# Layer 0's output stores on ScalarE's queue, and more yields between the steps of its attention

## The chip, the cores and the metric

The kernel runs on one core of a Trainium2 chip. The metric is the device time of one execution in microseconds; the time of a kernel is the median of several runs. One profiled execution goes with it, and its rows are in microseconds from the start of its span.

## What is computed

The input is `x` of shape 4 x 48 x 256 x 256 in float32. Four layers follow, each `x = x + layer(group_norm(x))`. Only layer 0 is touched by the change. Cut to what matters it is:

```python
qkv = conv1x1(gn(x), qkv_w)                 # 48 -> 144 channels
qkv = depthwise3x3(qkv, dw_w)
q, k, v = split(qkv)                        # each 48 x (256*256), one head
q, k = l2_normalize(q), l2_normalize(k)     # over the pixels
attn = softmax(q @ k.T * temperature)       # 48 x 48 for each image
x = x + conv1x1(attn @ v, proj_w)
```

Layer 1 is a set of recurrences along rows and columns, layer 2 and layer 3 are convolutions with 8 x 8 Fourier patches.

## The kernel before

Layer 0 never forms `q`, `k` or `v`. The 48 x 48 attention of an image depends only on correlations of the input with shifted copies of itself, so a first stage (the matmuls at L367 and L371) sums these over each image, and VectorE gathers statistics (L407). For each image a generator, `attention`, turns the sums into one small set of weights `wu[b]`: it contains `statistics` (matmuls `ps_mu`, `ps_va`, `ps_wt`), seven pairs of blocks (`ps_u`, `ps_y`), the reduction `half`, and small steps `ps_t`, `ps_l`, `ps_m`, `ps_w`, `ps_x` that end by writing `wu[b]`. Each `yield` in it is a place where other work may be put between two steps; the kernel's schedule is written out by hand, and instructions stand on each engine in the order in which the Python code issues them. One call of `next(steps)` runs the generator to its next yield. For images 0 to 2 the steps are spread between the matmuls of the next image's correlations, one call for every four column pairs, 64 calls for an image. Before the change the generator has 28 yields.

The last image has no next correlations. Its first steps run directly after the loop, and the rest runs in the output stage, one step after each row group.

The output stage applies `wu[b]` to the image as a 3 x 3 convolution in Winograd form over row pairs. It is 32 jobs, 8 for each image, each of 32 rows of the image in two halves `hf`:

- `load_out` (L459) brings the rows of a job into one of two buffers `xos`, two DMAs of 49 partitions x 18576 bytes, issued on SP two jobs ahead.
- `transform` (L475, L476, L478) is four pieces on GpSimd that write the tile `to` of the next job (two buffers).
- `out_rows`, four times in a job, makes two products of 48 matmuls each (`po`, L490, three buffers). ScalarE copies half of the first product to SBUF (`c2`, L502); VectorE adds and subtracts (L504, L505) and so empties that buffer; with the second product it finishes the rows (L507, L508) and gathers statistics for layer 1 (L510); four ScalarE copies (L514) put the rows into the stage tile of the job in layer 1's order.
- `store` (L523) writes the stage tile to the scratch tensor `x1` in four DMAs, each 48 channels x 64 runs of 128 bytes. They were issued on SP.

The order of issue in a job is: the loads for two jobs on, then for each of the four row groups one transform piece of the next job, one `out_rows` and one attention step of the last image (from job 1 on), and last the four stores. So on SP the loads of a job stand behind the stores of the job before.

Of the kernel before, what the change touches and what calls it, by code (L numbers as in the profile page):

```python
# [17 lines left out]
B, C, H, W = 4, 48, 256, 256  # L18
# [84 lines left out]
def layer0(k):  # L103
    nc, tc = k.nc, k.tc
    main, first, second = correlations()
    NB, CB = len(main) + len(first) + len(second), 5
    with ExitStack() as ctx:
# [5 lines left out]
        def small(name):  # L113
            return ps_s.tile([128, 512], F32, name=name, tag="small")
# [16 lines left out]
        with ExitStack() as gctx:  # L131
# [74 lines left out]
            def statistics(b, st):  # L206

                mv = sp.tile([128, C, 2], F32, name="mv", bufs=1)
                for c in range(C):
                    nc.vector.bn_aggr(mv[:, c, :], st[:, c].rearrange("p t s -> p (t s)"))  # L210
                    if c % 8 == 7:
                        yield
                ps = small("ps_mu")
                nc.tensor.matmul(ps[:, :C], ones, mv[:, :, 0], start=True, stop=True)
                groups = lambda x: x.rearrange("p (g i) -> p g i", i=3)
                gm = sp.tile([128, C // 3], F32, name="gm")
                nc.vector.tensor_reduce(gm, groups(ps[:, :C]), AX.X, ALU.add)
                nc.vector.tensor_scalar(gm, gm, 1.0 / 3, None, ALU.mult)
                spread = lambda x: x[:, :, None].broadcast_to([128, C // 3, 3])
                d = sp.tile([128, C], F32, name="dv")  # L220
                nc.vector.tensor_tensor(groups(d), groups(mv[:, :, 0]), spread(gm), ALU.subtract)
                nc.vector.tensor_tensor(d, d, d, ALU.mult)
                nc.vector.tensor_tensor(d, d, mv[:, :, 1], ALU.add)
                yield
                ps = small("ps_va")
                nc.tensor.matmul(ps[:, :C], ones, d, start=True, stop=True)
                gs = sp.tile([128, C // 3], F32, name="gs")
                nc.vector.tensor_reduce(gs, groups(ps[:, :C]), AX.X, ALU.add)
                nc.vector.tensor_scalar(gs, gs, 1.0 / 3, GN_EPS, ALU.mult, ALU.add)
                nc.scalar.activation(gs, gs, AF.Sqrt)  # L230
                nc.vector.reciprocal(gs, gs)
                nc.vector.scalar_tensor_tensor(gm, gm, -1.0, gs, ALU.mult, ALU.mult)
                for i, row in enumerate((gs, gm)):
                    full = sp.tile([128, C], F32, name="full")
                    nc.vector.tensor_copy(groups(full), spread(row))
                    dg = sp.tile([C, C], F32, name=f"dg{i}")
                    nc.vector.tensor_tensor(dg, k.ident[:C, :C], full[:C], ALU.mult)
                    if i == 1:
                        bias = sp.tile([C, 1], F32, name="bias")
                        nc.vector.tensor_reduce(bias, dg, AX.X, ALU.add)  # L240
                    for h in range(2):
                        if i == 0:
                            nc.vector.tensor_copy(lw[:, h * HP : h * HP + C], dg)
                        else:
                            nc.vector.tensor_copy(lw[:, h * HP + C : h * HP + CA], bias)
                yield
                ps = small("ps_wt")
                nc.tensor.matmul(ps[:, :P2], lw, wq, start=True, stop=True)
                wt = sp.tile([128, P2], F32, name="wt")
                nc.vector.tensor_copy(wt, ps[:, :P2])  # L250
                yield
                return wt

            def attention(b, st, pa, pb, pc):
# [5 lines left out]
                o = na + nb + 2 * na  # L260
                nc.vector.tensor_copy(cs[:HP, o : o + 4 * CA], pc[:HP, 2 * na : 2 * na + 4 * CA])
                wt = yield from statistics(b, st)
                edge = {"left": 13, "right": 13, "top": 16, "bottom": 16}

# [35 lines left out]
                half = sp.tile([P2, P2], F32, name="half")  # L300
                nc.vector.tensor_reduce(half, ws.rearrange("p m j -> p j m"), AX.X, ALU.add)
                yield
                ps = small("ps_t")
                nc.tensor.transpose(ps[:P2, :P2], half, k.ident[:P2, :P2])
                g = sp.tile([P2, P2], F32, name="g")
# [8 lines left out]
                nc.vector.reciprocal(rn, rn)  # L314
                nc.vector.tensor_scalar(gd, k.ident[:P2, :P2], rn, None, ALU.mult)
                yield
                ps = small("ps_l")
                nc.tensor.matmul(ps[:C, :C], g[:, :C], gd[:, C:], start=True, stop=True)
                at = sp.tile([C, C], F32, name="at")
# [5 lines left out]
                nc.vector.tensor_reduce(mx[:, 1:2], at, AX.X, ALU.add)  # L325
                nc.vector.reciprocal(mx[:, 1:2], mx[:, 1:2])
                nc.vector.tensor_scalar(at, at, mx[:, 1:2], None, ALU.mult)
                yield
                ps = small("ps_m")
                nc.tensor.matmul(ps[:C, :C], at, projT, start=True, stop=True)  # L330
# [82 lines left out]
            for at, (b, h, q) in enumerate(jobs):  # L413
                if at + 1 < len(jobs):
                    ts[at + 1] = load(*jobs[at + 1])
                if h == 0 and q == 0:
                    pa = ps_a.tile([128, 512], F32, name="pa")
                    pb = ps_b.tile([128, 512], F32, name="pb")
                    pc = ps_c.tile([128, 512], F32, name="pc")
                    st = rp.tile([128, C, 8, 6], F32, name="st", bufs=2)  # L420
                t = ts.pop(at)

                def step():
                    for i in range(8):
                        stats(st, h, q, t, range(6 * i, 6 * i + 6))
                        next(once if b == 0 else steps, None)
                        if b == 1:
                            next(once, None)
                        yield

                correlate(b, h, q, t, pa, pb, pc, step())
                if h == 1 and q == 3:
                    borders(pc, rw)
                    if b + 1 < B:
                        rw = load_border(b + 1)
                    steps = attention(b, st, pa, pb, pc)
                    next(steps)
            for _ in once:
                pass
            for _ in range(C // 8):  # L440
                next(steps)

        with ExitStack() as octx:
# [75 lines left out]
            def store(b, u, stage):  # L519
                for hf in range(2):  # L520
                    for c in range(2):
                        n0 = u * RU + hf * RU // 2 + c * RU // 4
                        nc.sync.dma_start(  # L523
                            k.x1[b // 2][:, b % 2, :, :, :, n0 : n0 + RU // 4, :].rearrange(
                                "c k p h n j -> c (k p h) (n j)"
                            ),
                            stage[c * HP : c * HP + C, hf].rearrange("c k p h n j -> c (k p h) (n j)"),
                        )
# [7 lines left out]
            for i, (b, u) in enumerate(jobs):  # L536
                cur = t
                if i + 2 < len(jobs):
                    xs[i + 2] = load_out(i, *jobs[i + 2])
                pieces = []  # L540
                if i + 1 < len(jobs):
                    t, pieces = transform(xs.pop(i + 1))
                for n in range(RU // 4):
                    if pieces:
                        pieces[n]()
                    out_rows(b, u, n, cur, stages[i % 2])
                    if i > 0:
                        next(steps, None)
                store(b, u, stages[i % 2])
# [1049 lines left out]
def network(ctx: ExitStack, tc: tile.TileContext, a):  # L1599
# [35 lines left out]
    k.y3 = [dp.tile([C, H, W], F32, name=f"y3_{b}") for b in range(B)]  # L1635

    layer0(k)
    layer1(k)
    layer2(k)
# [153 lines left out]
```

## Time and profile before

| what | us |
|---|---|
| median of 3 runs | 14373.09 |
| lowest and highest run | 14365.64 to 14403.29 |
| the profiled execution, its own time | 14317.74 |
| its span | 14316.0 |
| TensorE (PE) busy in the span | 13484.9 |
| VectorE (DVE) busy | 7589.3 |
| ScalarE (ACT) busy | 5440.0 |
| GpSimd (POOL) busy | 4000.5 |
| layer 0: correlations | 0 to 1266 |
| layer 0: output stage, first to last product | 1297.85 to 2082.99 |

An engine's busy time counts its compute instructions; issuing a DMA is not counted, so ScalarE or SP can be held up without appearing busy. A row of a timeline gives the start, the duration, the engine, the line of the kernel, the operation with its output and inputs, how many, and in brackets how long the engine was idle before and what ended that. SPq is SP's issuing queue. A line of a table of windows gives the stretch, its length, the busy time and number of instructions of PE, weight loads, DVE, ACT and POOL, the granted TensorE clock, and the DMA engines' share and GB/s.

### The profile page before, as it was taken

What the parts mean: (1) busy time and instruction counts of PE and PEld (TensorE: products, weight loads), DVE (VectorE), ACT (ScalarE), POOL (GpSimd) and SP (SyncE); (2) the same over time, 40 slices, a digit from 0 to 9 for tenths busy, and PEclk for the clock granted to TensorE, in tenths of its full rate; (3) what the DMA queues carried; (4) which work ended last, traced back from release to release, by engine and by line L of the source; (5) the groups of instructions that cost most, each with busy time, mean ns of one, the idle gap of its engine ahead of it and who ended that gap; (6) DMA issues with size and microseconds to landing.
All of it is one profiled execution on the core that took longest, in us unless ns stands there. A gap on an engine that the chain in (4) does not pass through costs nothing.

```text
span 14316.0 us, 409316 instructions
## 1 busy us (share of the span) xinstructions
PE 13484.9 (94%) x177348; PEld 9066.8 (63%) x177348; DVE 7589.3 (53%) x18639; ACT 5440.0 (38%) x11419; POOL 4000.5 (28%) x3769
## 2 busy tenths in 40 slices
PE   9998979999999899999999999997999999899998
PEld 5555657676767655555555555555777777666666
DVE  2334753333545566666666666664555555565554
ACT  0001334422320055555555555553444444232232
POOL 0002760000006544444444444441111111111111
PEclk9999989999999999999999999996999898898888
DMA  3333677766659833333333333325887777787787
GB/s 145 145 145 106 141 138 132 129 149 145 151 145 222 193 44 46 45 46 47 44 48 47 47 48 46 46 40 112 166 166 161 156 162 159 159 167 150 154 161 142
DMA packets 1843543, 1681.08 MB, mean 117 GB/s; under 512 B 1486821, under 2 KB 1588586, under 8 KB 1804634
## 3 DMA queue, kind: packets, MB, share of 16 engines
q1 hardware_dynamic: 1776202, 1378.92, 44.8%
q0 software_dynamic: 65536, 275.97, 12.1%
q8 instruction: 1393, 22.82, 0.8%
q14 instruction: 412, 3.38, 0.1%
HBM read 978.44 MB, written 676.01 MB: 116 GB/s over the span
## 4 chain that ended last, share of the span: by engine, by line
PE 79%; DVE 8%; DMA 6%; issue 3%; POOL 2%; ACT 1%; SPq 1%; DVEq 0%; POOLq 0%; ACTq 0%
PE pc L959 17%; PE p L610 16%; PE pg L1437 8%; PE pb L371 6%; PE py L1365 5%; PE pm L1402 4%; PE pm L1483 4%; PE pa L990 3%; PE pm L1458 3%; PE pb L1015 3%; DMA xo<-in_x_p 2%; PE pm L1340 2%; PE pb L1069 2%; PE pb L1060 2%; PE pa L367 2%
## 5 line engine op out<-in xcount | busy, mean ns | idle before, releaser
L959 PE MATMUL pc<-wg,t 50*64 50x288 f32 x49152 | 3373.3, 405 | 151.7 <-DVE qkv L975 113.2
L959 PEld LDWEIGHTS pc<-wg,t 50*64 50x64 f32 x49152 | 2010.9, 133 | 1459.2 <-issue 318.0
L1377 DVE TENSOR_TENSOR z<-py,meff 64x288 f32<-64x288 f32 x4096 | 1687.6, 451 | 1121.0 <-PE py L1365 1095.4
L1437 PE MATMUL pg<-z,kw 100*64 100x64 f32 x36864 | 1486.9, 238 | 144.6 <-DVE gall L1450 80.1
L1437 PEld LDWEIGHTS pg<-z,kw 100*64 100x64 f32 x36864 | 1336.4, 148 | 347.8 <-issue 158.7
L1053 POOL TENSOR_TENSOR z<-z,gb 128x768 f32<-128x768 f32 x512 | 933.4, 1823 | 2101.4 <-ACT z L1047 1584.7
L610 PE MATMUL p<-carry,wk_down 96*96 96x256 f32 x6120 | 1356.2, 384 | 94.9 <-DVE carry L615 54.9
L975 DVE TENSOR_TENSOR qkv<-pc,c 128x576 f32<-128x576 f32 x1024 | 773.1, 755 | 1230.5 <-ACT c L974 1210.3
L610 PEld LDWEIGHTS p<-carry,wk_down 96*96 96x96 f32 x6120 | 1010.0, 165 | 440.7 <-DVE carry L615 67.8
L778 POOL TENSOR_TENSOR x1in<-carry,x1in 96x256 f32<-96x256 f32 x512 | 435.1, 855 | 2413.3 <-DMA x1in<-x 2215.6
L371 PE MATMUL pb<-t 128*64 128x490 f32 x4096 | 1041.5, 576 | 7.4 <-DMA t<-in_x_t 7.4
L982 DVE TENSOR_TENSOR qkv<-pc,qkv 128x576 f32<-128x576 f32 x1024 | 773.6, 755 | 337.2 <-PE pc L959 309.3
L1450 DVE TENSOR_TENSOR gall<-gall,pg 128x384 f32<-128x384 f32 x768 | 426.0, 555 | 861.9 <-PE pg L1437 654.4
L1365 PE MATMUL py<-wi,xf 48*64 48x144 f32 x16384 | 836.5, 321 | 45.8 <-issue 24.2
L490 PE MATMUL po<-to,wu 49*64 49x256 f32 x12288 | 711.6, 391 | 57.9 <-POOL to L475 50.8
L1415 POOL DMA_DIRECT2D z<-eb x256 | 130.0, 508 | 2245.5 <-DMA eb<-yb 958.1
L908 ACT ACTIVATE xn<-xr,ab 48x1152 f32<-48x1152 f32 (+1 forms) x512 | 716.7, 1428 | 29.7 <-DMA xr<-x 24.8
L1463 ACT COPY gt<-pm 100x512 f32<-100x512 f32 x1024 | 544.4, 591 | 481.8 <-PE pm L1458 479.3
L1402 PE MATMUL pm<-z,mb 64*32 64x396 f32 x6144 | 701.0, 556 | 12.3 <-issue 10.3
L1365 PEld LDWEIGHTS py<-wi,xf 48*64 48x64 f32 x16384 | 536.6, 146 | 264.4 <-issue 148.0
L1448 ACT ACTIVATE gall<-pg 128x384 f32<-128x384 f32 x768 | 378.3, 493 | 854.2 <-PE pg L1437 844.2
L610 PE MATMUL p<-carry,wk_left 96*96 96x256 f32 x3060 | 668.8, 381 | 34.4 <-DVE carry L615 34.4
(213 smaller groups left out, 19427.5 us busy)
## 6 DMA issues: line engine op xcount, KB each, us to landing
t<-in_x_t SPq DMA_DIRECT2D x96, 1666.0 KB
eb<-yb SPq DMA_DIRECT2D x1024, 148.5 KB
z<-eb POOLq DMA_DIRECT2D x512, 297.0 KB, 10.4
xf<-xf SPq DMA_DIRECT2D x512, 224.0 KB
xo<-in_x_p SPq DMA_DIRECT2D x64, 888.9 KB
xr<-x SPq DMA_DIRECT2D x120, 432.0 KB
x<-stage SPq DMA_DIRECT2D x128, 384.0 KB
xin<-x SPq DMA_DIRECT2D x128, 384.0 KB
```

Source lines behind the costliest of these rows:

```text
L371: nc.tensor.matmul(out, left, right, **flags)
L490: nc.tensor.matmul(p[c * HP : (c + 1) * HP, hf, i], wu[b][o, m, dx], t[o, m, c * NP // 2 + n, dx : dx + W], start=(dx == 0), stop=(dx == 2),)
L610: nc.tensor.matmul(pv, wk[name][:, o, :], old[:, :, o : o + N], start=(o == 0), stop=(o == 2))
L908: lambda up=up, rows=rows, half=half, wp=wp, dst=dst, dm=dm, m0=m0, m1=m1: nc.scalar.activation(rows[:, dst, wp, m0 - dm : m1 - dm], src[: ...
L959: nc.tensor.matmul(pc[cc * HP : (cc + 1) * HP, h, :O], j.t[p, which, n, w0 : w0 + HP], wg[p, which, dx], start=(dx == 0), stop=(dx == 2),)
L975: nc.vector.tensor_tensor(j.qkv[:, g // 2, :, g % 2], j.pc[1][:, 0:1, :O].broadcast_to([128, 2, O]), c2, ALU.add)
L982: nc.vector.tensor_tensor(o, j.pc[0][:, :, :O], o, ALU.add)
L1053: nc.gpsimd.tensor_tensor(z, z, gb[:, i : i + 1, :].broadcast_to([128, 8, Q]), op)
L1365: nc.tensor.matmul(py[v * HP : (v + 1) * HP, hf, ii * PASS : (ii + 1) * PASS], xf[p, i, v, :], wi[p, j.ps, :], start=True, stop=True,)
L1377: nc.vector.tensor_tensor(out[:, :, :, v, :], py[p, hf, : 2 * PASS].rearrange("p (i c e) -> p c i e", i=2, e=2), meff[p, j.ps].rearrange(" ...
L1402: nc.tensor.matmul(pb[32 * q : 32 * q + 32, :n], mb, z[:, a : a + n], start=True, stop=True)
L1437: nc.tensor.matmul(pg[e * HP : (e + 1) * HP, kk], k.k3[g][:, (t * GP + kk) * 2 + e, :], z[:, :, t * NP2 + g * GP + kk, :, e], start=True, ...
```

## The change

Two edits. The four stores of a job are issued on ScalarE's queue instead of SP's, in the same place of the program, so behind the last stage copies of the job and ahead of the first copy of the next. And six bare `yield` lines are added to the generator: one ahead of `ps_va`, two ahead of `ps_wt`, one each ahead of `ps_t`, `ps_l` and `ps_m`, so 34 in all; the loop after the correlations runs five steps instead of six, so that `ps_mu` goes into the output stage. From `store` on, line numbers of the changed kernel are higher by 6.

```diff
@@ statistics
                 nc.vector.tensor_tensor(d, d, mv[:, :, 1], ALU.add)
                 yield
+                yield
                 ps = small("ps_va")
...
+                yield
+                yield
                 yield
                 ps = small("ps_wt")
@@ attention
                 yield
+                yield
                 ps = small("ps_t")
...
                 yield
+                yield
                 ps = small("ps_l")
...
+                yield
                 yield
                 ps = small("ps_m")
@@ after the correlations
-            for _ in range(C // 8):
+            for _ in range(C // 8 - 1):
                 next(steps)
@@ store
-                        nc.sync.dma_start(
+                        nc.scalar.dma_start(
                             k.x1[b // 2][:, b % 2, :, :, :, n0 : n0 + RU // 4, :].rearrange(
```

## The prediction

> **What bounds the kernel now.** I read the page for the weight of layer 0 (the lines of layers 1 to 3 are untouched), then the chain that ended last, to find who sets the pace of layer 0's output stage, then SP's issues, one row of the stage in order of time, and the places where TensorE stops. The stage runs from the first product at 1297.85 us to the end of the last at 2082.99: 785.1 us for 32 jobs.
>
> The chain between 1700 and 2030 us (start, length, what) is a loop over the loads of `xo`:
>
> ```profile
> 1706.70 15.90 DMA xo<-in_x_p
> ...
> 2020.75 15.81 DMA xo<-in_x_p
> ```
>
> Between these two lie 13 periods, 314.05 / 13 = 24.2 us per job. TensorE itself needs less, as its column in the table of windows shows (494.95 of 530 us busy, part of that at a slow clock):
>
> ```profile
> 1510.00:2040.00 530.00, 494.95 (x8636) 345.16 (x8632) 347.69 (x542) 190.60 (x453) 385.48 (x259) 0.95 0.64 143
> ```
>
> SP's issues in order of time (start, length held, line, count):
>
> ```profile
> 1369.22 9.80 SPq L523 DMA_DIRECT2D x<-stage  x4
> ...
> 1707.10 21.94 SPq L523 DMA_DIRECT2D x<-stage  x4
> 1729.14 3.12 SPq L459 DMA_DIRECT2D xo<-in_x_p  x2
> 1732.36 19.67 SPq L523 DMA_DIRECT2D x<-stage  x4
> 1752.13 3.09 SPq L459 DMA_DIRECT2D xo<-in_x_p  x2
> ```
>
> The reader is to see that SP is never free: 3.12 + 19.67 us and small gaps make the whole 23 us from 1729.14 to 1752.13. A store moves 3072 runs of 128 bytes, and its issue is long by itself:
>
> ```profile
> L523 SPq DMA_DIRECT2D x<-stage x128: 302/3037/16118, 1323.5 to 2091.4; - x128
> ```
>
> Minimum, median and maximum: the first of four is taken in 0.33 us, each later one waits 3.04 for the one before, and one per job waits 13 to 16 behind the load just issued on the same queue. Without a load ahead four stores hold the queue 9.80 us (at 1369.22). That number is the core of this forecast.
>
> One row of the stage while nothing is short (four rows make a job):
>
> ```profile
> 1735.21 0.59 ACT L502 COPY c<-po 112x512 f32<-112x512 f32 x1 [0.22 <-PE po L490]
> 1735.83 0.69 DVE L504 TENSOR_TENSOR y<-po,c 112x512 f32<-112x512 f32 x1 [0.66 <-ACT c L502]
> 1736.44 0.68 DVE L505 TENSOR_TENSOR y<-po,c 112x512 f32<-112x512 f32 x1
> 1737.75 0.69 DVE L507 TENSOR_TENSOR y<-po,y 112x512 f32<-112x512 f32 x1 [0.63 <-PE po L490]
> ...
> 1738.47 0.43 ACT L514 COPY stage<-y 112x256 f32<-112x256 f32 x1 [2.68 <-DVE y L507]
> 1739.07 1.10 ACT L514 COPY stage<-y 112x256 f32<-112x256 f32 x3 [0.16 <-DVE y L508]
> ...
> 1740.39 0.59 ACT L502 COPY c<-po 112x512 f32<-112x512 f32 x1 [0.23 <-PE po L490]
> ```
>
> L502 to L502 is 5.18 us, so a half-row product takes 2.59 and a job 20.72. ScalarE idles only 0.2 us between the last stage copy (ends 1740.17) and the next L502, and L502 is what lets VectorE empty a `po` buffer. Two more places, a restart of TensorE after a stop, and the longest stall in the last image's attention:
>
> ```profile
> 1723.91 6.63 PE L490 MATMUL po<-to,wu 49*64 49x256 f32 x60 [3.75 <-POOL to L475]
> ...
> 1729.43 0.59 ACT L502 COPY c<-po 112x512 f32<-112x512 f32 x1 [6.82 <-PE po L490]
> ```
>
> ```profile
> 1329.68 20.53 DVE L229 TENSOR_SCALAR gs<-gs 128x16 f32<-128x16 f32 x1
> ...
> 1352.46 0.74 PE L248 MATMUL ps_wt<-wq,lw 48*128 48x96 f32 x2 [19.90 <-DVE lw L245]
> ```
>
> After a stop of 3.75 us, 60 matmuls take 6.63 us, 0.110 each instead of 0.054: the first product ends 5.52 us after the restart instead of 2.59, so a stop costs about 3.0 us on top of itself.
>
> **The change, part by part.** *Stores to ScalarE.* On SP it removes 19.7 to 21.9 us of issue per job. The loads then go out as soon as GpSimd has read the old buffer, about 18 us into a job (4 pieces of 1.10 + 1.10 + 2.39 us), land 14 to 16 us later, and are wanted at the start of the job after next: off the path. Taken alone the period would fall from 24.2 to TensorE's 20.72.
>
> On ScalarE it adds 4 issues per job behind the last stage copy. Queued behind them: the next job's first L502; behind that VectorE's L504 and L505 (in order, so all its later work), and TensorE, which has three `po` buffers. With the end of the job's last product as zero: L507 starts at 0.05, the last stage copy ends at 0.05 + 2.42 = 2.47 (rows above), four stores hold ScalarE 9.80 us to 12.3, L502 starts there instead of at 2.59, and L505 ends 1.91 later (1735.21 to 1737.12), at 14.2. TensorE fills three buffers by 3 x 2.59 = 7.8 and stops until 14.2: 6.4 us. With the slow restart of 3.0 that is 9.4 per job. The rest of the job catches up: at half speed ScalarE and VectorE have 5.5 us for a half-row that takes them 2.6. Period 20.7 + 9.4 = 30.1. Of 32 jobs 31 have a successor to delay: 31 x 9.4 = 292 us.
>
> No row shows an issue on ScalarE. The near row is the same store on SP, 9.80. From below: each is taken in 0.33 as the first of four is, 1.3 us in all, and costs nothing, because the third buffer leaves 3.3 us of slack (12.3 - 2.59 = 9.7 of delay made 6.4 of stop). From above: ScalarE also waits for the fourth store's runs, 9.80 + 3.04 = 12.8, which gives 12.4 per job, 385 us. I take 9.80: same transfer, same runs.
>
> The Trainium skill, "Perfetto Trace Analysis", section "DMA Instruction — HWDGE (DVE, Sync)", says that the issuing sequencer is held until all descriptors of its DMA have been generated; the 0.33 us of the first store speaks for one that is generated after the issue returned, and by the page alone the term would be the 385. "DMA: Bandwidth & Descriptors", section "Issuing engines are not separate DMA queues", says that issuing from several engines saves only the sequencer's issue time, usually small next to the transfer; here that time is 19.7 of 23 us, so the page's "small" does not hold, and by its words the change would be worth nothing.
>
> Would stores still wait for loads, as on SP (19.67)? At a period of 30 us a load goes out at 18 and lands at 32 to 34, so 2 to 4 us into the next job; the stores start at 2.5 and end at 15. They hardly meet, and the longer the period the less. I price this at 0, at most 2 us per job.
>
> *The spacing.* The edited generator serves all images. For images 0 to 2, 34 yields instead of 28 fit the 64 slots; TensorE is busy all through them (320.0 of the 320 us from 400 to 720 us) and other matmuls stand between the steps either way: 0. Dropping one step after the loop saves nothing, as TensorE idles from 1266.4 to 1297.85 for the `xo` buffers, not for `ps_mu`. In the output stage the third image's steps spread over 29 rows instead of 22. Their matmuls stay: about 13 us. Now TensorE stops 19.9 us (above), 2.5 for `half` and 4.0 for the `wu` chain, with three slow restarts 35 us. L229 took 0.175 us elsewhere and here 20.53, until GpSimd's unbroken run of `to` pieces ended. With three steps between, `ps_wt` no longer waits; but the same kind of operation (L218) now stands in job 1, at about 1341, with GpSimd busy to 1350. I put 18 us, between 5 (all hidden) and 35 (as now).
>
> **Sum for the stage:** 663.0 (32 x 20.72) + 3 (first slow start) + 13 + 18 + 292 = 989, against 785: +204 us. The tail stays: the last four stores leave at the same distance from the last row, SP or ScalarE. On the profiled execution's 14317.74 us (span 14316.0) this is 14522. That execution lies 55 us below the median of the three runs, 14373.09; on that median, 14577.
>
> **The rivals.** *Faster:* ScalarE is not held by its issues. Then the stage is 663 + 3 + 13 + 35 (GpSimd busy 18 of 20.7 us, so the lock stays) = 714, 71 us less: 14302. For it: the 0.33 us of the first issue. Against it: 3.04 is the median, with nothing else ahead. It decides below a hold of some 6 us: break-even is (785 - 697) / 31 = 2.8 us per job beyond the 3.3 of slack. *A longer hold:* the fourth store counts, or stores meet the tail of a load: 989 + 93 = 1082, 14670. With every store behind a load (19.67) it would be 31 x 19.3 = 598 and 14880, but the loads' phase, above, excludes that for most jobs. *Nothing to measure:* a hold of 5 to 6 us, where the unblocked loads pay for ScalarE's stops; about 14373. No row lies there.
>
> **How the numbers follow.** The forecast (hold near 9.8) has 0.72, the longer hold 0.14, no change 0.04, faster 0.10. A comparison of this kernel resolves some 0.3%, 43 us. The likeliest case spans +100 to +270: the stall term between 6.5 (a restart without slow clock) and 11 us per job, and 5 to 35 for the attention. The range reaches into the longer hold, 14465 to 14690, and leaves the faster case out.
>
> **What would show it.** Right: ScalarE issues of 3.0 us, three of four, with the store line on the chain; TensorE stopping about 6 us in every job, ended by VectorE's L511 (today's L505); granted clock in the stage well under 0.95; no wait of GpSimd for `xo`; period near 30 us. Wrong: issues of 0.3 us on ScalarE and a period of 21, or an L508 that starts on time; or issues of 13 us there, which would mean that loads and stores collide again.

## The result and the profile after

| what | before | after |
|---|---|---|
| median of 6 runs, us | 14388.19 | 14592.06 |
| lowest to highest, us | 14338.89 to 14457.49 | 14530.67 to 14618.88 |
| span of the profiled execution, us | 14316.0 | 14545.3 |
| layer 0's output stage, us | 785.1 | 960.8 |

The ratio of the times is 1.0128, 95% interval 1.0091 to 1.0165: slower by more than the 0.3% that such a comparison resolves. The stage now runs from 1297.4 to 2258.2 us and is 175.7 us longer. The span is 229.3 us longer; the other 54 us lie outside the stage, in code that the change does not touch. The span without the stage was 13530.9 us before and 13584.5 after, and between 13504.4 and 13637.1 in the ten kernels below, which have the same code there. It varies by some 130 us from one execution to the next, so the length of the stage is the sharper measure here, and the medians the fairer one of the whole.

The table of windows over the stage, first of before, then of after, shows what became of TensorE (columns: stretch, length, busy time and number of PE, weight loads, DVE, ACT, POOL, granted clock, DMA share, GB/s):

```profile
1297.00:2083.00 786.00, 723.63 (x12433) 508.04 (x12433) 534.22 (x811) 273.89 (x648) 572.67 (x384) 0.94 0.61 136
```

```profile
1297.00:2258.00 961.00, 766.30 (x12435) 542.52 (x12435) 505.49 (x815) 270.78 (x648) 570.31 (x384) 0.87 0.48 111
```

The same instructions take 43 us more of TensorE's time, because the clock is 0.87 instead of 0.94, and TensorE idles 194.7 us instead of 62.4. So 132 of the 175 us are stops and 43 are slow clock.

The chain of waits of after, at the last job boundary (start, length, what):

```profile
2230.05 0.33 ACT stage L520
2230.38 2.90 ACTq L529
2233.28 0.04 issue
2233.32 3.17 ACTq L529
2236.50 0.03 issue
2236.53 3.08 ACTq L529
2239.61 0.04 issue
2239.65 0.59 ACT c L508
2240.27 0.69 DVE y L510
2240.96 0.61 DVE y L511
2241.57 0.14 issue
2241.71 16.51 PE po L496 x240
```

Where the loop over the `xo` loads was, there now stands ScalarE's own queue: the last stage copy, three stores of 2.90 to 3.17 us, then the L508 that had to wait for them, L510 and L511 on VectorE, and TensorE's restart. The product before it had ended at 2235.66, so TensorE stood still for 6.04 us.

The issues of after show who holds what (shortest, median and longest in ns, first and last start):

```profile
L529 ACTq DMA_DIRECT2D x<-stage x128: 309/3042/15111, 1322.9 to 2266.6; - x128
L465 SPq DMA_DIRECT2D xo<-in_x_p x64: 269/270/557, 1282.0 to 2158.6; - x64
```

The store costs ScalarE the same 3.04 us that it cost SP. SP is free now: its loads are issued in 0.27 us. The hold of an ordinary boundary on the timeline:

```profile
1758.76 0.31 ACTq L529 DMA_DIRECT2D x<-stage  x1
1759.11 9.47 ACTq L529 DMA_DIRECT2D x<-stage  x3
```

That is 0.31 + 9.47 and a small gap, 9.82 us. From 1589 us on TensorE stops 5.7 to 6.8 us once in every job, 5.95 at the median, and the mean period is 29.4 us.

### The profile page after: what moved, and what is told of

It is laid out like the page before. It is cut to its first block, busy times and chain, and to the rows that moved or that the text cites. A ratio compares the mean times of both kernels' runs of the same rounds, so it can differ in the third digit from the quotient of the medians.

```text
span 14545.3 us, 409219 instructions
## 1 busy us (share of the span) xinstructions
PE 13563.4 (93%) x177348; PEld 9154.4 (63%) x177348; DVE 7552.5 (52%) x18639; ACT 5436.9 (37%) x11419; POOL 4001.7 (28%) x3769
## 4 chain that ended last, share of the span: by engine, by line
PE 69%; DVE 6%; DMA 4%; issue 2%; ACT 1%; SPq 1%; POOL 0%; ACTq 0%; DVEq 0%; POOLq 0%
PE pc L965 18%; PE p L616 16%; PE pg L1443 8%; PE py L1371 5%; PE pm L1408 4%; PE pm L1489 3%; PE pa L996 3%; PE pm L1464 3%; PE pb L1021 3%; PE pm L1346 2%; PE pb L1075 2%; PE pb L1066 2%; DVE p L1012 2%; DMA z<-eb 1%; DVE qkv L981 1%
## 5 line engine op out<-in xcount | busy, mean ns | idle before, releaser
L496 PE MATMUL po<-to,wu 49*64 49x256 f32 x12288 | 754.6, 407 | 225.8 <-DVE y L511 131.7
L496 PEld LDWEIGHTS po<-to,wu 49*64 49x64 f32 x12288 | 530.3, 145 | 442.1 <-issue 126.5
L914 ACT ACTIVATE xn<-xr,ab 48x1152 f32<-48x1152 f32 (+1 forms) x512 | 716.8, 1429 | 29.4 <-DMA xr<-x 24.5
## 6 DMA issues: line engine op xcount, KB each, us to landing
z<-eb POOLq DMA_DIRECT2D x512, 297.0 KB, 10.4
```

The costliest lines, as they stand in the source:

```text
L496: nc.tensor.matmul(p[c * HP : (c + 1) * HP, hf, i], wu[b][o, m, dx], t[o, m, c * NP // 2 + n, dx : dx + W], start=(dx == 0), stop=(dx == 2),)
L914: lambda up=up, rows=rows, half=half, wp=wp, dst=dst, dm=dm, m0=m0, m1=m1: nc.scalar.activation(rows[:, dst, wp, m0 - dm : m1 - dm], src[: ...
```

## The experiments

### Each half of the change alone

The stores alone, on the kernel before:

```diff
-                        nc.sync.dma_start(      # store
+                        nc.scalar.dma_start(
```

> Before with the four stores of a job on ScalarE and no added yields. Theory (ScalarE is held about 9.3 us by three of four issues, TensorE stops about 6 us and restarts at half clock in each job): output stage, first to last product, 950 to 985 us against 785 before and 961 with the whole change, period 29.6 us per job, total 1.0 to 1.4% above before. Rival (the spacing of the steps makes the loss): stage near 785, total within 0.3% of before.

Measured: median 14508.75, ratio 1.0124 (1.0073 to 1.0176); stage 965.2 us, period mostly 28.4 to 30.3. The whole loss is in this line.

The spacing alone (stores on SP):

```diff
-                        nc.scalar.dma_start(    # store of the changed kernel
+                        nc.sync.dma_start(
```

> The added yields alone, stores on SP as before. Theory: SP still sets the pace of 24.2 us per job, stage 760 to 790 us, total within 0.3% of before; the one long VectorE stall (20.5 us) may go or move. Rival (the spacing makes the loss): stage 900 to 960 us, total 1% slower.

Measured: median 14326.12, ratio 0.9988 (0.9963 to 1.0013); stage 788.6 us against 785.1. The spacing makes no difference that can be measured. The profile says why: the long operation of VectorE did not vanish, it moved. Before, L229 stood 20.53 us. In this kernel L218 does (four of them, one for each image; the last is the long one):

```profile
L218 DVE TENSOR_SCALAR gm<-gm x4: 174/174/20708, 391.5 to 1329.4; 128x16 f32<-128x16 f32 x4
```

Either way VectorE stands until GpSimd's unbroken run of `to` pieces ends: L229 ended at 1350.21 and the last piece at 1350.18, here L218 at 1350.16 and the piece at 1350.13. TensorE stands with it.

### The size of the hold

If the hold follows from the 3072 short runs of a store, then fewer and longer runs with the same bytes must shorten it. First 48 runs of 8 KB:

```diff
+                        at = (u * 4 + hf * 2 + c) * 2048
                         nc.scalar.dma_start(
-                            k.x1[b // 2][:, b % 2, :, :, :, n0 : n0 + RU // 4, :].rearrange(
-                                "c k p h n j -> c (k p h) (n j)"
-                            ),
-                            stage[c * HP : c * HP + C, hf].rearrange("c k p h n j -> c (k p h) (n j)"),
+                            k.x1[b // 2][:, b % 2].rearrange("c k p h n j -> c (k p h n j)")[:, at : at + 2048],
+                            stage[c * HP : c * HP + C, hf].rearrange("c k p h n j -> c (k p h n j)"),
```

> The whole change, but each store writes one run of 8 KB per channel instead of 64 runs of 128 bytes (same bytes, so the pixels of x1 land in another order and what layer 1 computes from them is not layer 1). Theory (the hold is the time to generate runs): issues of 0.3 us on ScalarE, no stop of TensorE at the job boundary, period 20.7 to 21.5, stage 680 to 725 us. Rival 1 (an issue on ScalarE is dear whatever it moves): issues of 3 us and a stage near 960. Rival 2 (loads and stores on two queues slow each other): period stays above 24.

Measured: median 14295.84, ratio 0.9950 (0.9922 to 0.9978); stage 734.6 us, a little above the expected 725, periods of 20.7 to 21.7 us from job 9 on with one of 22.4. The issues and one boundary on the timeline:

```profile
L530 ACTq DMA_DIRECT2D x<-stage x128: 308/516/2766, 1321.9 to 2035.2; - x128
```

```profile
1714.33 0.31 ACTq L530 DMA_DIRECT2D x<-stage  x1
1714.68 3.30 ACTq L530 DMA_DIRECT2D x<-stage  x3
1718.02 0.59 ACT L508 COPY c<-po 112x512 f32<-112x512 f32 x1 [3.06 <-DMA x<-stage]
```

Four stores still hold ScalarE for 3.7 us here, but L508 comes no later than TensorE's spare `po` buffer allows, and TensorE does not stop. Over jobs 10 to 30 the hold is 3.4 to 5.3 us, 3.85 at the median, part of it a wait for an earlier DMA on the same semaphore (the counter that tells of a landing) to land; the eight longest holds, from 4.3 us up, bring stops of 0.4 to 1.4 us. With the stores on ScalarE and short to issue, the moved stores pay: the loads no longer set the pace. The excess over 725 is job 1, with a period of 43.7 us: here L218 stood from 1331.81 to 1348.48, again to the end of GpSimd's run.

Then half way, 1536 runs of 256 bytes:

```diff
+                        at = (u * 2 + hf) * 4096
+                        d = k.x1[b // 2][:, b % 2].rearrange("c k p h n j -> c (k p h n j)")[:, at : at + 4096]
                         nc.scalar.dma_start(
-                            k.x1[b // 2][:, b % 2, :, :, :, n0 : n0 + RU // 4, :].rearrange(
-                                "c k p h n j -> c (k p h) (n j)"
+                            d.rearrange("c (r t x) -> c r t x", t=2, x=64)[:, :, c],
+                            stage[c * HP : c * HP + C, hf].rearrange("c k p h n j -> c (k p h n j)").rearrange(
+                                "c (r x) -> c r x", x=64
                             ),
-                            stage[c * HP : c * HP + C, hf].rearrange("c k p h n j -> c (k p h) (n j)"),
```

> The whole change, but each store writes runs of 256 bytes, so 1536 instead of 3072 (same bytes, so the pixels of x1 land in another order and what layer 1 computes from them is not layer 1). Theory (1 us per 1000 runs; ScalarE held by three of four issues): issues of 1.5 us, hold 4.9 us, TensorE stops 1 to 1.5 us per job, period 21.9 to 23.4, stage 735 to 790 us. Rival (hold does not scale with runs): period above 26.

Measured, one run: 14430.02; stage 862.2 us, periods of 22.5 to 29.4 from job 10 on, most near 26.7. The size was missed; the timeline of one boundary shows by how much:

```profile
1724.56 0.31 ACTq L531 DMA_DIRECT2D x<-stage  x1
1724.91 6.30 ACTq L531 DMA_DIRECT2D x<-stage  x3
1733.30 24.14 PE L496 MATMUL po<-to,wu 49*64 49x256 f32 x384 [2.82 <-DVE y L511]
```

An issue takes about 2.1 us and not half of 3.04, so the hold is 6.65 us, and that makes a stop of 2.82 us with a slow restart behind it. The kernels line up, and not only at these boundaries. Take the hold from the start of the first store's issue to the end of the last, at the 84 boundaries from job 10 to 30 in the changed kernel, the stores alone, the 256-byte and the 8 KB runs. The 13 holds of up to 3.88 us bring no stop. For the other 71, from 4.26 to 10.58 us, the stop is the hold less 3.84 us, within 0.03 us in all but one. So each microsecond beyond 3.84 us of slack is a microsecond of stop, to which the restart is added.

### The slow restart

To separate the stop from the clock, matmuls into PSUM that nobody reads were put into the place where TensorE stops, from job 10 on:

```diff
+                if n == 1 and b * NJ + u >= 10:
+                    fill = [small("ps_f") for _ in range(2)]
+                    for i in range(24):
+                        for hf in range(2):
+                            o = slice(hf * HP, hf * HP + CA)
+                            for c in range(2):
+                                nc.tensor.matmul(
+                                    fill[hf][c * HP : (c + 1) * HP, :W],
+                                    wu[b][o, 0, 0], t[o, 0, c * NP // 2 + n, :W],
+                                    start=(i == 0), stop=(i == 23),
+                                )
```

> The whole change, and from job 10 on 96 matmuls of the products' shape, into PSUM that nobody reads, stand between the two half-row products of the second row, where TensorE stops: they add 5.2 us of work to every job from 10 on. Theory (a stop of 6 us costs about 3 us more because the granted clock is halved when work returns): the filler takes the place of the stop, the clock stays at 1.00, and the period falls from 29.4 to 26.5 to 27.5 us although work was added. Rival (the slow matmuls after the stop come from something else, or the stop is not the cause of the loss): period 29.4 or more.

Measured, one run: 14542.08; stage 996.0. I had mis-sized the filler: each of these float32 matmuls stands as two instructions on TensorE, so it was 192 of them and 10.4 us in every job, not 5.2. It more than filled the gap, the period became exactly 20.7 + 10.4 = 31.1 us, and the window shows TensorE without a microsecond of idle time at full clock:

```profile
1700.00:2200.00 500.00, 500.00 (x9272) 498.71 (x9267) 247.71 (x388) 135.53 (x325) 286.20 (x192) 1.00 0.48 112
```

(The 48 matmuls of a product in the trace are, for the same reason, 24 of the program.) That shows no price of the clock yet. With half of it (12 rounds instead of 24, 96 instructions):

> As the first filler run, with half of it: from job 10 on 96 TensorE instructions (5.2 us at full clock, one row's worth) stand where TensorE stops, which leaves a stop of some 0.7 us. Theory (the halved clock after a stop costs 2.8 us per job): clock 1.00, period 29.4 - 2.8 = 26.6 us, stage 900 to 912 us although 5.2 us of work were added to 22 jobs. Rival (the stop alone is the loss): period 29.4.

Measured, one run: 14562.59; stage 923.7, a little over what was expected, since four of the jobs took 28.4 to 31.3 us; the others from job 10 on took 26.7 to 27.6. So a job with 5.2 us of useless work added is 2.3 us shorter than the 29.4 without it. The windows from 1700 to 2200 us, first of the changed kernel, then with the filler, give the clock as 0.87 and 0.99:

```profile
1700.00:2200.00 500.00, 398.57 (x6544) 281.50 (x6540) 261.24 (x410) 141.95 (x341) 303.73 (x206) 0.87 0.49 114
```

```profile
1700.00:2200.00 500.00, 477.21 (x8672) 419.71 (x8668) 274.08 (x432) 149.02 (x360) 315.63 (x211) 0.99 0.53 118
```

In 18 of the 22 jobs the stop that is left is 0.5 to 1.5 us and costs no slow restart; the four longer jobs are those with stops of 1.8 to 3.5 us, and three of these stops were followed by the slow clock. The halved clock after a stop of 5.9 us costs 2.3 us a job by this comparison (29.4 - 27.1) and 2.8 by the period (29.4 - 20.7 - 5.9); the prediction had 3.0.

### Other places for the stores

If ScalarE has 3.8 us of slack after each row group as it has at the job boundary, one store there should be free:

```diff
+                    if i > 0:
+                        store(*jobs[i - 1], stages[(i - 1) % 2], n)    # one of the four
                     out_rows(b, u, n, cur, stages[i % 2])
...
-                store(b, u, stages[i % 2])
+            for s in range(4):
+                store(*jobs[-1], stages[(len(jobs) - 1) % 2], s)
```

> The whole change, but the four stores of a job are issued on ScalarE one at a time, one ahead of each row group of the next job (the last job's four at the end). Theory (an issue waits only for the runs of the issue before it, 3 us, and a row lasts 5.2 us): every issue about 0.3 us, no stop at the boundary, period 20.7 to 21.5, stage 680 to 730 us, total 0.4 to 0.8% below before. Rival (the generator holds ScalarE through its own store): each issue 3 us, ScalarE 8.6 + 12 us per job, period 21 to 24. Rival (contention of two queues): period above 24.

Measured: median 14461.64, ratio 1.0086 (1.0057 to 1.0116); stage 855.5 us. The expectation failed: it is slower than before. The issues and one job on the timeline:

```profile
L528 ACTq DMA_DIRECT2D x<-stage x128: 309/310/10811, 1320.0 to 2158.1; - x128
```

```profile
1799.28 1.00 SPq L465 DMA_DIRECT2D xo<-in_x_p  x2
1802.09 0.31 ACTq L528 DMA_DIRECT2D x<-stage  x1
1807.27 6.78 ACTq L528 DMA_DIRECT2D x<-stage  x1
1814.15 0.59 ACT L508 COPY c<-po 112x512 f32<-112x512 f32 x1 [5.81 <-PE po L496]
```

The median issue is 0.31 us, as hoped. But 26 of them take 5.4 to 10.8, nearly one for each pair of loads, and that is the second store after the loads have gone out on SP (20 times) or the first (6 times). The store issued at 1802.09 is not through 5 us later, where 3.04 is enough with no load about; the next one waits for it, L508 behind that. The loads hold up the stores from another queue too. The packets say until when: in 23 of the 26 the long issue ends 0.67 to 0.75 us after the last 18576-byte packet of the loads (here 1814.05 after 1813.4).

The mirror image, loads on ScalarE and stores back on SP, spacing as changed:

```diff
-                    nc.sync.dma_start(      # load_out
+                    nc.scalar.dma_start(
...
-                        nc.scalar.dma_start(    # store
+                        nc.sync.dma_start(
```

> The queues swapped: the two xo loads of a job on ScalarE, the four stores back on SP, yields as in the whole change. Theory (an issue blocks only the queue it stands on; generating runs waits while a load is in flight, whichever queue holds the load, as one store per row showed): ScalarE is held 0.6 us per job, no stop from it; SP needs about 9.5 us of runs plus up to 14 of waiting on loads, so the period lies between 20.7 and 24.2, stage 700 to 780 us, 10 to 80 us faster than before. Rival (two queues do not block each other at all): period 20.7, stage 690. Rival (a load is slowed by the stores beside it until GpSimd waits): period above 24.2.

Measured: median 14413.29, ratio 1.0013 (0.9986 to 1.0040); stage 820.8 us, above the expected 700 to 780. Periods jump between 20.7 and 28 to 33 us: a load on ScalarE is cheap, but on SP one store in nearly every job waits 12.8 to 16.1 us, in 26 of 29 cases to 0.7 us after the last packet of the loads, and now the stage buffer comes free too late. Waits of the stretch from 1600 to 2000 us (total, times, longest):

```profile
ACT stage L520 <- DMA x<-stage: 77.5, 7, 12.2
POOL to L481 <- PE po L496: 106.7, 11, 15.2
```

Two stores on each queue:

```diff
-                        nc.scalar.dma_start(
+                        (nc.sync, nc.scalar)[hf].dma_start(
```

> The whole change, but two stores of a job (the first half of the rows) on SP again and two on ScalarE. Theory (ScalarE waits for the runs of one store instead of three; loads and stores still share the DMA engines): hold on ScalarE 3.4 us without a load in flight, up to 7 beside SP's stores or a load, against some 3.9 of slack; TensorE stops 0 to 3 us, period 21 to 25 us, stage 700 to 810 us, total between 0.5% below and 0.2% above before. Rival (any issue on ScalarE costs as four do): period 29, stage 950.

Measured: median 14454.06, ratio 1.0067 (1.0037 to 1.0096); stage 859.5 us, outside the 700 to 810. Two stores beside each other slow each other: the waiting one takes 3.3 to 5.2 us on SP and 5.2 to 6.4 on ScalarE after job 0, and the loads stand behind SP's again, for which GpSimd waits, up to 12.4 us at a time and 206.1 in the stage.

Last, the loads themselves. In the kernel before, each was split, on the reasoning that a load of 48 partitions spreads over all 16 DMA engines and one of 49 over fewer:

```diff
+                    for c0, c1 in ((0, C), (C, CA)):
                         nc.sync.dma_start(
-                            x[hf * HP : hf * HP + CA].rearrange("c r w -> c (r w)"),
-                            k.x_p[b, :, r0 : r0 + RU + 2, :].rearrange("c r w -> c (r w)"),
+                            x[hf * HP + c0 : hf * HP + c1].rearrange("c r w -> c (r w)"),
+                            k.x_p[b, c0:c1, r0 : r0 + RU + 2, :].rearrange("c r w -> c (r w)"),
```

> Before (stores on SP, no added yields), with each xo load of 49 partitions issued as one of 48 partitions and one of 1. The same bytes. Theory (49 partitions are spread over 7 of the 16 DMA engines, 48 over 16, so a load lands in 5 to 7 us instead of 14, and the store behind it on the queue waits that much less): SP per job 9.8 + 3 + 5 to 7, under TensorE's 20.7; period 20.7 to 21.5, stage 690 to 735 us, total 0.3 to 0.7% below before. Rival (the load takes 14 us for its bytes, however it is split): period stays 24.2.

Measured: median 14405.9, ratio 1.0012 (0.9985 to 1.0039); stage 824.0 us, 39 longer than before. The theory fell and the rival held, as the same stretch of before and of this kernel shows:

```profile
1600.00:2000.00 400.00, 369.72 (x6348) 249.86 (x6344) 253.92 (x396) 138.63 (x330) 298.16 (x201) 0.94 0.65 142
```

```profile
1600.00:2000.00 400.00, 359.51 (x6144) 295.41 (x6140) 246.70 (x385) 134.85 (x320) 287.71 (x193) 0.93 0.93 138
```

The DMA engines are busy 0.93 of the time instead of 0.65, and move 138 GB/s instead of 142. A packet of 18576 bytes takes 2.09 us at the median over the stage instead of 0.70. The spread worked: while a job's two loads run, 13.3 to 14.0 such packets are in flight on average instead of 5.8 to 6.6. But the data came no sooner: the 98 packets of a pair take 13.3 to 14.6 us where they took 12.6 to 15.4. What limits the load was not found.

## Why the prediction was right, and where its terms were off

**What held.** Slower, and inside the range: 14577 predicted, 14592 measured. That the two agree to 15 us is partly luck: in the profiled pair the stage grew by 176 us where the sum had 204, and time outside it, in which the forecast had no change, varies by some 130 us from execution to execution. The mechanism is the one forecast, and the stores alone bring it (965.2 against 960.8 us). The price taken from SP's rows, 9.80 us for four stores, was 9.82 on ScalarE; the issues are 0.31 and three times 3.04. The chain runs through the stores, L508 and L511. SP no longer sets the pace, and GpSimd waited for `xo` only once, for 10.4 us, at the opening of the stage. The lower bound (issues cost nothing on ScalarE), and with it the faster rival, is excluded by the 3.04; the upper one (ScalarE waits for its fourth store too, 385 us) by L508 starting right after the third of the waits. The break-even lies between a hold of 3.85 us, faster than before, and one of 6.65, with a longer stage. The working that put it near 6 us charged the stop alone and left out the slow restart that the forecast charges; a straight line between the two stages (734.6 and 862.2 us) crosses 785 at 5.0 us, which is an estimate.

**The size.** The stage was 961 us where the sum had 989. The stall term was 31 x 9.4 = 292; the steady period of 29.4 makes it 29.4 - 20.7 = 8.7 a job, 270 us. The stop is 5.9 instead of 6.4, because the first store is already taken while the last stage copies finish, so the hold ends earlier than their end plus 9.80. Counted from the first issue, which starts 0.64 us before the last stage copy ends, the slack is 3.84; the prediction, counting from the end of that copy, had 3.3. The restart is 2.3 to 2.8.

**The page on the hold.** By the Trainium skill, "Perfetto Trace Analysis", section "DMA Instruction — HWDGE (DVE, Sync)", the sequencer is held until all descriptors of its own DMA have been generated; with the 3.04 us of the rows for each store, an estimate by it is 12.8 us. After's rows decide against it: 9.82, with L508 starting 0.04 us after the last of the four issues.

**Job 1 came out right for another reason.** I had 18 us for the attention, with L218 waiting for GpSimd in job 1. In the changed kernel L218 took 0.175 us. What stood there was ScalarE, held through the same stretch by the stores of job 0, as the timeline shows:

```profile
1323.31 24.34 ACTq L529 DMA_DIRECT2D x<-stage  x3
1332.01 18.61 SPq L465 DMA_DIRECT2D xo<-in_x_p  x4
1347.69 0.59 ACT L508 COPY c<-po 112x512 f32<-112x512 f32 x1 [24.13 <-DMA x<-stage]
```

One of the three took 15.1 us. In this job the loads go out while the stores are being issued, so here the collision happened that I had priced at 0 for every job. VectorE, whose queue was blocked behind L508, reached L218 at 1352.25, when GpSimd's run was over (1349.73). Where ScalarE was not held so long, L218 did stand in job 1, for 20.7 us (spacing alone) and 16.7 (long runs). So job 1 takes 43.7 to 45.4 us in these three kernels, whichever of the two is in front.

The Trainium skill, "SBUF — State Buffer", section "SBUF: two separate sides", says that VectorE and GpSimd share one pair of ports, which whoever starts first holds for the whole instruction while the other blocks; of VectorE's instructions it counts those in a 2-port mode, or with two inputs in SBUF against a GpSimd instruction that reads SBUF. L218 has one input, and no run here shows its mode. The rows agree that VectorE is blocked, but a single GpSimd piece is 1.1 to 2.4 us long, and the wait lasted through a whole run of them.

**The collision in the steady jobs.** There my 0 was right, for the reason given: at a period of 29.4 us, loads and stores pass each other. But it holds only because the kernel became slow. Other placements lose it. With one store per row group the loads are in the stores' way again (issues of 5.4 to 10.8 us); with the loads on ScalarE the stores on SP wait for them; with two and two the stores of the two queues slow each other, and the loads stand behind SP's. In each case that took back what the shorter hold had gained. This is why none of the three other placements beat the kernel before.

**What stays open.** Why a store's issue waits for a load of another queue was not settled. It waits for the load's packets, to 0.7 us after the last of them, and not for a semaphore: the DMA that had last used the store's semaphore had landed before each of the 26 long issues with one store per row group began. That loads and stores share the DMA engines is the reading that fits, but no run here separates it. The version that the runs point to, stores with long runs, needs another order of `x1` and a layer 1 that reads it; it was not built, so its 0.9950 is what layer 0 would gain, with whatever layer 1's reads would then cost left out.

## What to carry to other kernels

A DMA with thousands of short runs costs its issuing engine time for every issue that follows (3.04 us here); read that from the rows of the issues before moving it, and set it against the slack of the engine that gets it, not against that engine's busy share (ScalarE had only 271 us of work in 961). Moving stores away from the loads frees the loads, but whoever takes the stores pays with what is queued behind them; the cure is fewer and longer runs, not another queue. And a stop of TensorE of some 2 us or more mostly costs more than its length here, since the matmuls after it run at half the clock.

## What the runs showed of the hardware

- The issue is not proportional to the runs: for the same bytes an issue behind another store takes 3.1 us with 3072 runs, 2.1 with 1536 and 1.0 with 48 (means of jobs 10 to 30).
- A store on ScalarE's queue waits for loads on SP's queue (issues of 5.4 to 10.8 us with one store per row group, 15.1 in job 1 of the changed kernel), in most cases to 0.7 us after the loads' last packet. In before, with both on SP, all 26 long issues end 0.8 us after it. A load's issue on SP beside stores on ScalarE takes 0.27 us at the median and 1.6 at most.
- Spreading a load over more DMA engines did not make it faster: 138 GB/s against 142, with packets three times as long.
- Whether TensorE restarts slowly depends on the length of the stop. Over the output stage of the twelve traces, none of the 79 stops of 0.4 to 1.5 us was followed by a granted clock of 0.5 within 7 us, 62 of the 79 from 1.5 to 3.2 us were, and all 154 longer ones. The Trainium skill, "TensorE: Matmul & The Clock Gate", section "Part 1: The HAM clock gate", says that the clock halves after an idle window of about 3.4 us; the 62 shorter stops show that less is often enough in these runs.
